# Two float32 additions of a recurrent graph layer moved from VectorE to TensorE, in a kernel whose instruction order is planned by searched leads

## The chip, the cores and the metric

The kernel runs on one core of a Trainium2 chip. The core has a tensor engine (PE, which multiplies matrices into PSUM), a vector engine (DVE), a scalar engine (ACT), GpSimd (POOL), and a sync engine (SP), which here only issues DMAs. Each engine works through its own queue in order; they wait for one another by semaphores. The metric is the device time of one execution in microseconds, lower is better. A profile of one execution gives the start and the duration of the instructions, the waits, and the clock that was granted to PE.

## The reference

Sixteen graphs of 1024 nodes with 64 features go through four layers, each of the form `x = x + layer(relu(layernorm(x)))`:

```python
# layer 0: two dense layers, a product with adj, and a recurrent (GRU) cell
msg = relu(adj @ m)
r, z = sigmoid(i_r + h_r), sigmoid(i_z + h_z)
n = tanh(i_n + r * h_n)
x = x + (1 - z) * n + z * h
# layer 1: normalized adjacency (adj + I), a dense layer, relu
# layer 2: each node's neighbours are thinned out by rank, and per feature a weighted sum
#          of three quantiles over the neighbours left is taken; then two dense layers
# layer 3: (adj + I) @ h, divided by the row sums
```

Layer 2 is the costly one: per node and feature the values of its neighbours have to be gathered and sorted. The change is in the last line of layer 0. With `h` the normalized input, the kernel computes it as `X + (n + z * (h - n))`.

## The kernel before

One graph is held as 8 tiles of 128 nodes. Python generators, one per stage and graph, issue the instructions. The stages are: `fetch` and `load` (read the adjacency, transpose it on PE, copy it to SBUF on ACT, write the transpose `adjT` to DRAM, take its signs), `code`, `rank`, `cut`, `list` (find degrees, rank the nodes by degree, thin the neighbours out, and make lists of neighbour indices), `mid` (layer 0, function `dense0`), `next` (layer 1, `dense1`, which ends by writing the table `tab` of normalized features to DRAM), `gath` (POOL's indirect DMAs fetch the neighbours' rows from `tab`), `sort` (sorting networks of minima and maxima on DVE for the 128 nodes of highest degree), `smalls` and `sums` (the same in two groups for the other seven tiles), and `rear` (`dense23`: the rest of layer 2, and layer 3).

POOL's gathers carry three names. The 26 `gh` gathers of a graph fetch the heavy nodes' neighbours into four buffers that come free only when PE has transposed them (`bank<-ident,gh`). The 49 `s` gathers (and 2 `px`) fill the light groups. The 8 `zz` gathers of the rear fetch a graph's aggregate `agg` back in node order; they stand in POOL's queue among the `s` gathers of the next graph, and wait until that graph's sorted sums are written. The `gh` gathers need the list `idxH` (a CAST on DVE) and the table `tab`.

The order of all this is written out by a planner, class `Order`. It keeps a clock per engine, a cost per instruction, and for each waiting stage the time at which its next step could start; the stage with the earliest start goes next. To that start a *lead* is added, in microseconds, from the table `LEAD`: per kind of stage five numbers for the engines V, A, T, P, S, one per graph index, and some for the first and the last graphs. The leads decide which stage's instructions come first in an engine's queue, and they come from a search. Since every queue is in order, an instruction that waits holds up all that stands behind it on its engine.

PSUM is handed out as four banks of 128x512 (`bank()`) and two double ones. A stage takes a bank, fills it from PE, and closes it when it is evicted.

All engine instructions are recorded through one helper, so the profile gives them all line 465; they are told apart by the names of their tiles: `hm` is `h` of layer 0, `nn` is `n`, `rz` holds `r` and `z`, `X` is the running `x` of the graph. The change is at the end of `dense0`. Around it:

```python
            yield "A", nn
            A.activation(nn, nn, AF.Tanh)
            yield "V", nn

            V.tensor_sub(h, h, nn)
            V.tensor_mul(h, h, rz[:, :, H : 2 * H])
            V.tensor_add(h, h, nn)
            V.tensor_add(X, X, h)
```

The first reader of the new `X` is `layernorm_relu` in `dense1`, which begins with a sum over the features on DVE (`ln_sn<-X`).

Of the kernel before, what the change touches and what calls it, by code (L numbers as in the profile page):

```python
# [156 lines left out]
def in_two_buffers(lens, kept, moves, first=None):  # L157
# [62 lines left out]


LEAD = {
    "rear": ((-0.25, -0.25, 0.25, -11, -65.5), -0, (0, -0, -0, -0), (-0.75, -6.5)),
    "gath": ((-11, 0, 0, -4.5, 0.25), -0, (-1.5, -0, 0, 0), (0, -0.25)),
    "sums": ((0, 0, 4, 21.75, -163.5), 0, (-0.75, 0, -0.75, 0), (0, 21.25)),
    "next": ((0, 0, 0, 14, 1.25), -0, (-0.5, 0, -0, 0), (0, 0)),
    "mid": ((0, -0, 0, 1, 4), 0, (-1, 0, -0, 0), (-0, 0)),
    "code": ((-192, -107.5, -0.25, 10, 0), 0, (5, 0, 1, -2), (3, 0)),
    "rank": ((0, 0, -121.5, 9.5, 7.75), 0, (-3.25, 0, 0, -0), (0, 0)),
    "cut": ((0, -1.25, -95.25, 0, -83.75), 0, (0, 0, 0, 0), (0, -0)),  # L230
    "list": ((-0, -3.5, -1, -10, -33.5), 0, (1, 0, -0, 0), (0, 0)),
    "fetch": ((-68.25, -2.25, -21.25, -29.5, -149.75), 0, (-10.5, -31.25, 0, -1.75), (2, 16)),
    "load": ((-49.75, 0, -163, -2.75, 1.25), 0, (-7.75, -0.5, 0, 0), (1, 1)),
    "sort": ((0, -79.5, -0.5, 21.25, -30.5), -0, (0, 0, 0, 0), (0.25, -0.75)),
    "smalls": ((0, 12.25, 7.5, 1.25, 1.5), 0, (0, 0, 0, 0), (-1.75, 1)),
    "flag": ((4, -17, -4.25, -1.75, -4.5), 0.1, (0, 8.5, 0, -8), (0, 0.75)),
    "keep": ((23, -0.75, 32.5, 4.25, -26), -1.55, (-9.75, -22.25, 7.25, 3.5), (15, 3.75)),
    "stream0": ((6, 0, 0, 2.5, -14.75), -0.15, (-9.25, 16.75, 0, 7.5), (-2.25, 2)),
    "stream1": ((8.75, -6, 11.25, 13.25, -2), 0.1, (3.5, 2.25, 0.75, -13.75), (-4.5, -5.75)),
    "stream3": ((-2.75, -4.75, -23, 1.75, -52.5), 1.5, (0.5, 0.5, 0, -6.25), (-27, -8.5)),  # L240
}


# [227 lines left out]
def kernel(  # L471
# [38 lines left out]
    ident = const.tile([P, P], F32, name="ident")  # L510
# [88 lines left out]
    def lists_for_all():  # L599
        order = Order(B)  # L600
        V, A, T = Engine(nc.vector, "V", order), Engine(nc.scalar, "A", order), Engine(nc.tensor, "T", order)
        G_, S_ = Engine(nc.gpsimd, "P", order), Engine(nc.sync, "S", order)

        def pool(name, bufs, **kw):
            return Pool(main.enter_context(tc.tile_pool(name=name, bufs=bufs, **kw)), order, bufs)
# [3 lines left out]
        ps1 = pool("ps1", 4, space=bass.MemoryType.PSUM)  # L609
        ps2 = pool("ps2", 2, space=bass.MemoryType.PSUM)  # L610

        def bank(dtype=F32):
            return ps1.take([P, 512 * 4 // mybir.dt.size(dtype)], dtype, "bank")
# [54 lines left out]
        for k in range(8):  # L668
            v = NBITS * 2.0**k
# [675 lines left out]
        def layernorm_relu(X, h=None, who="m", times=None):  # L1345

            yield "V", X
            s = wp.tile([P, NT], F32, name="ln_s" + who, bufs=2)
            V.reduce_sum(s, X, AX.X)
            yield "A", s  # L1350
            v = wp.tile([P, NT], F32, name="ln_v" + who, bufs=2)
            if h is None:
                h = wp.tile([P, NT, H], F32, name="h" + who, tag="h2r" if who == "r" else None, bufs=1)
            for t in range(NT):
                A.activation(h[:, t, :], X[:, t, :], AF.Square, bias=s[:, t : t + 1], scale=-float(H), accum_out=v[:, t : t + 1])
            A.activation(v, v, AF.Sqrt, bias=eps, scale=1.0 / H**3)
            yield "V", v
            V.reciprocal(v, v)
            if times is not None:
                V.tensor_mul(v, v, times)  # L1360
            V.scalar_tensor_tensor(s, s, -1.0 / H, v, ALU.mult, ALU.mult)
            yield "A", s, v
            for t in range(NT):
                A.activation(h[:, t, :], X[:, t, :], AF.Relu, bias=s[:, t : t + 1], scale=v[:, t : t + 1])
            return h
# [15 lines left out]
        def both(name, tag):  # L1381
            return wp.tile([P, N // 2], F32, name=name, tag=tag)

        def beside(on):
            T.beside = bool(on)

        def transposed(h, dst):
            yield "T", h
            pt = yield from bank()
            for t in range(4):  # L1390
                T.transpose(pt[:, t * P : (t + 1) * P], pair(h, t), ident)
            yield "A", pt
            for i in range(2):
                A.copy(dst[:, i * 512 : (i + 1) * 512], pt[i * H : (i + 1) * H, :])
            ps1.close(pt)
# [61 lines left out]
        def evicted(pm, dst, func=AF.Copy, bias=0.0):  # L1457
            yield "A", pm
            A.activation(dst, pm, func, bias=bias)
            ps1.close(pm)  # L1460
# [7 lines left out]
        def dense0(b, S):  # L1468
            S["X"] = X = wp.tile([P, NT, H], F32, name="X", bufs=2)
            S_.dma_start(X, x[b].rearrange("(t p) h -> p t h", p=P))  # L1470

            h = yield from layernorm_relu(X)
            cat = wp.tile([P, N], F32, name="cat")
            yield from transposed(h, cat[0:H, :])
            yield "T", cat
            m1T = both("m1T", "big")
            pm = yield from bank()
            for i in range(2):
                beside(i)
                T.matmul(  # L1480
                    pm[i * H : (i + 1) * H, :], w1, cat[0:H, i * 512 : (i + 1) * 512], start=True, stop=True
                )
            beside(0)
            yield from evicted(pm, m1T, AF.Relu, b1d)
            yield "T", m1T
            yield after(f"load{b}")
            p2 = yield from bank()
            T.matmul(p2, *bias(0), start=True, stop=False)
            ams = streamed(b, 0)
            for t in range(4):  # L1490
                T.matmul(
                    p2[:, t * P : (t + 1) * P], m1T[:, t * P : (t + 1) * P], w2d, start=False, stop=t == 3
                )
            yield "A", p2
            A.activation(m2x, p2.rearrange("p (t h) -> p t h", h=H), AF.Relu)
            ps1.close(p2)
            ps = yield from bank()
            pm = yield from propagated(b, m2x, 0, ams, sums=ps)

            yield "A", ps  # L1500
            m1T = wp.tile([P, 256], F32, name="sT", tag="big")
            A.copy(m1T, ps[:, 0:256])
            ps1.close(ps)
            yield "A", pm
            for i in range(2):
                A.activation(cat[H:P, i * 512 : (i + 1) * 512], pm[i * H : (i + 1) * H, :], AF.Relu)
            ps1.close(pm)
            yield "T", m1T
            pr = yield from bank()
            for c in range(2):  # L1510
                T.matmul(pr[:, c:NT:2], m1T[:, c * P : (c + 1) * P], pick, start=True, stop=True)
            yield "V", pr
            S["rs"] = rs = st.tile([P, NT], F32, name="rs")
            V.tensor_scalar(rs, pr[:, 0:NT], 1.0, None, ALU.add)
            ps1.close(pr)
            rz = wp.tile([P, NT, 2 * H], F32, name="rz", tag="big")
            nn = t2("nn")
            for g in range(2):
                yield "T", cat
                pg = yield from bank2()  # L1520
                for i in range(4):
                    t = 4 * g + i
                    o = pg[:, i * 4 * H : (i + 1) * 4 * H]
                    if i % 2 == 0:
                        T.matmul(pg[:, i * 4 * H : (i + 2) * 4 * H], *bias(2), start=True, stop=False)
                    c = (t % 2 * 4 + t // 2) * P
                    T.matmul(o, cat[:, c : c + P], wg, start=False, stop=i % 2 == 1)
                pgv = pg.rearrange("p (i c) -> p i c", c=4 * H)
                gs = slice(4 * g, 4 * g + 4)
                yield "A", pg  # L1530
                A.activation(rz[:, gs, :], pgv[:, :, 0 : 2 * H], AF.Sigmoid)
                yield "V", rz
                V.tensor_mul(nn[:, gs, :], pgv[:, :, 2 * H : G], rz[:, gs, 0:H])
                V.tensor_add(nn[:, gs, :], nn[:, gs, :], pgv[:, :, G : 4 * H])
                ps2.close(pg)
# [3 lines that stand above are left out]

            V.tensor_sub(h, h, nn)  # L1540
            V.tensor_mul(h, h, rz[:, :, H : 2 * H])
            V.tensor_add(h, h, nn)
            V.tensor_add(X, X, h)

        def dense1(b, S):
            X, rs = S["X"], S["rs"]
# [631 lines left out]
    ps1 = ctx.enter_context(tc.tile_pool(name="ps1", bufs=2, space=bass.MemoryType.PSUM))  # L2178
# [363 lines left out]
```

## Time and profile before

| | |
|---|---|
| median of 7 runs | 2278.94 us (2268.46 to 2289.73) |
| profiled execution | 2278.91 us, its span 2276.7 us |
| mean granted PE clock | 0.764 |
| DVE, ACT, POOL, PE busy | 84%, 68%, 67%, 67% of the span |
| first gather to last `s` gather | 155.1 to 2214.4 us from the span's start |

The span runs from the first to the last instruction of the profiled execution; the 2.2 us between it and that execution's time lie around it. An engine's busy share counts instructions that ran, not the time in which it issued a DMA or waited. In a line of a group the columns are: line, engine, operation, output and inputs with their shapes and the number of instructions, then busy time in all and mean nanoseconds of one, then the idle time just before them and what ended it. In a line of waits: who waited, for whom, microseconds in all, how often, and the longest. Numbers at the end of a tile's name are left out.

### The profile page before, as it was taken

Reading aid. Unit: us, or ns where it says so; the run is one execution under the profiler, and the core shown is the slowest. Engines: PE = TensorE matmul, PEld = TensorE weight load, DVE = VectorE, ACT = ScalarE, POOL = GpSimd, SP = SyncE. Lnnn points to the kernel's source line nnn. Section 1 sums busy time; section 2 is a strip of 40 time slices with the busy share of each in tenths; the row PEclk is TensorE's granted clock in tenths of the full one; section 3 lists DMA queues with packets and bytes.
Section 4 is the critical chain, followed back from the end, with each engine's and each line's share of the span. In section 5 each row is a group of like instructions: output and inputs, shape, how many; then the busy total and the mean of one; then the engine's idle time right before and its main releaser. Section 6 shows DMA issues by size and latency. Waiting matters only on the chain. (4 is left out here: it accounts for less than half of the span.)

```text
span 2276.7 us, 35564 instructions
## 1 busy us (share of the span) xinstructions
PE 1514.6 (67%) x9522; PEld 789.7 (35%) x9522; DVE 1907.2 (84%) x6317; ACT 1537.4 (68%) x5241; POOL 1519.0 (67%) x1428
## 2 busy tenths in 40 slices
PE   4876757676757677687876767766767685763324
PEld 3433334333333433333433433333333333331112
DVE  3547898898898988988997899888889899888982
ACT  5877776787777677787787668767866677554221
POOL 5017767567776776767676777677777677777771
PEclk9888778787678869797877787877777676775665
DMA  6767657677757667677767766766756565352341
GB/s 203 230 201 211 196 150 197 203 200 226 203 147 238 190 176 211 201 231 227 222 183 202 203 201 192 223 176 209 204 153 204 168 196 165 111 169 80 102 147 25
DMA packets 402724, 419.80 MB, mean 184 GB/s; under 512 B 176236, under 2 KB 313330, under 8 KB 402514
## 3 DMA queue, kind: packets, MB, share of 16 engines
q1 hardware_dynamic: 357426, 372.68, 53.1%
q0 software_dynamic: 45088, 44.75, 9.2%
q8 instruction: 78, 1.28, 0.2%
q14 instruction: 132, 1.08, 0.2%
HBM read 332.94 MB, written 84.34 MB: 183 GB/s over the span
## 5 line engine op out<-in xcount | busy, mean ns | idle before, releaser
L465 POOL DMA_INDIRECT s<-tab,idxL x784 | 863.8, 1102 | 239.0 <-issue 228.6
L465 POOL DMA_INDIRECT gh<-tab,idxH x416 | 445.0, 1070 | 343.9 <-DMA tab<-h 116.7
L465 DVE TENSOR_TENSOR hb<-hb 128x128 f32<-128x128 f32 (+10 forms) x1040 | 522.8, 538 | 16.3 <-ACT hb L465 11.7
L465 PE MATMUL bank<-ident,a 128*128 128x128 f32 x1024 | 196.5, 331 | 108.1 <-DMA a<-in_adj_dram 54.7
L465 POOL DMA_INDIRECT zz<-agg,posi x128 | 144.2, 1127 | 122.0 <-issue 47.2
L465 PE MATMUL bank<-am,tr 128*64 128x512 f32 x512 | 170.8, 780 | 74.0 <-ACT tr L465 37.1
L465 PE MATMUL bank<-am,hr 128*64 128x512 f32 x480 | 160.5, 777 | 74.5 <-ACT hr L465 41.7
L465 PE MATMUL bank<-am,m2x 128*64 128x512 f32 x512 | 165.5, 730 | 52.8 <-DMA am<-adjT 49.5
L465 PEld LDWEIGHTS bank<-ident,a 128*128 128x128 f32 x1024 | 143.2, 170 | 160.5 <-issue 46.6
L465 ACT COPY strip<-bank 128x512 f32<-128x512 f32 x256 | 146.6, 591 | 55.5 <-PE bank L465 43.5
L465 DVE TENSOR_TENSOR hb<-hb,hb 128x488 f32<-128x488 f32 (+7 forms) x368 | 173.4, 483 | 4.5
L465 ACT ACTIVATE s<-s,wl 128x64 f32<-128x64 f32 x624 | 166.5, 348 | 9.6 <-DVE s L465 9.6
L465 ACT ACTIVATE junk<-bank,nkey 128x1024 bf16<-128x1024 f32 x128 | 142.3, 1111 | 28.4 <-PE bank L465 26.2
L465 ACT ACTIVATE sgn<-strip,flat 128x1024 bf16<-128x1024 f32 x128 | 147.5, 1152 | 4.9 <-PE bank L465 1.8
L465 PE MATMUL bank<-cx,oh 128*128 128x133 f16 (+1 forms) x1280 | 143.2, 262 | 7.7 <-DVE oh L465 6.6
L465 PE MATMUL bank<-ident,gh 128*128 128x128 f32 x208 | 65.1, 340 | 120.0 <-DMA gh<-tab,idxH 103.7
L465 PEld LDWEIGHTS <-oh 128*128 128x128 f16 x1280 | 97.0, 109 | 47.0 <-issue 17.2
L465 DVE TENSOR_TENSOR o<-s 128x64 f32<-128x64 f32 (+6 forms) x208 | 95.1, 489 | 17.8 <-ACT s L465 10.4
L465 PE MATMUL bank<-wg,cat 128*128 128x256 f32 x256 | 94.2, 502 | 0.0
L465 DVE TENSOR_TENSOR s<-o 128x192 f32<-128x192 f32 (+5 forms) x224 | 94.0, 447 | 0.0
L465 PE MATMUL bank<-am,ones 128*32 128x256 f32 x1024 | 92.8, 438 | 0.0
L465 PEld LDWEIGHTS bank<-ident,gh 128*128 128x128 f32 x208 | 30.7, 158 | 175.8 <-issue 129.1
(443 smaller groups left out, 3742.9 us busy)
## 6 DMA issues: line engine op xcount, KB each, us to landing
am<-adjT SPq DMA_DIRECT2D x376, 512.0 KB
a<-in_adj_dram SPq DMA_DIRECT2D x128, 512.0 KB
adjT<-strip SPq DMA_DIRECT2D x128, 512.0 KB
s<-tab,idxL POOLq DMA_INDIRECT x784
gh<-tab,idxH POOLq DMA_INDIRECT x416
wb<-wd SPq DMA_DIRECT2D x32, 152.0 KB
X<-in_x_dram SPq DMA_DIRECT2D x16, 256.0 KB
x<-X SPq DMA_DIRECT2D x16, 256.0 KB
```

What stands on the lines that cost most here:

```text
L465: return f(*args, **kw)
```

## The change

The last two additions are no longer done on DVE. The stage waits until `X`, `nn` and `h` are ready for PE, takes a bank, and multiplies the identity with each of the three 128x512 tiles in turn, in float32, all three accumulated in that bank. ACT then copies the bank over `X`, and the bank is closed. The leads were searched anew, so the order of nearly everything else differs too: all 18 rows of `LEAD` have new numbers.

```diff
 LEAD = {
-    "rear": ((-0.25, -0.25, 0.25, -11, -65.5), -0, (0, -0, -0, -0), (-0.75, -6.5)),
-    "gath": ((-11, 0, 0, -4.5, 0.25), -0, (-1.5, -0, 0, 0), (0, -0.25)),
+    "rear": ((-0.25, -0.25, 0.25, -54, -111.25), 0, (0, -0, 0, 0), (-9, 1.5)),
+    "gath": ((-23, 0, 0, -8.5, 0), 0, (0, -1.5, 0, -0), (0.5, -1.25)),
...
-    "list": ((-0, -3.5, -1, -10, -33.5), 0, (1, 0, -0, 0), (0, 0)),
+    "list": ((0, -3.5, 0, -10.5, -95.75), 0, (0.75, 0, 0, -0), (0, 1.25)),
...
             V.tensor_sub(h, h, nn)
             V.tensor_mul(h, h, rz[:, :, H : 2 * H])
-            V.tensor_add(h, h, nn)
-            V.tensor_add(X, X, h)
+            yield "T", X, nn, h
+            px = yield from bank()
+            for i, v in enumerate((X, nn, h)):
+                T.matmul(px, ident, v.rearrange("p t h -> p (t h)"), start=i == 0, stop=i == 2)
+            yield "A", px
+            A.copy(X.rearrange("p t h -> p (t h)"), px)
+            ps1.close(px)
```

## The prediction

> **What bounds the kernel now.** I read the page first. No engine is full: DVE is busy for 84% of the span, the other three for about two thirds.
>
> ```profile
> span 2276.7 us, 35564 instructions
> PE 1514.6 (67%) x9522; PEld 789.7 (35%) x9522; DVE 1907.2 (84%) x6317; ACT 1537.4 (68%) x5241; POOL 1519.0 (67%) x1428
> ```
>
> POOL's share misleads, so the groups of instructions came next.
>
> ```profile
> L465 POOL DMA_INDIRECT s<-tab,idxL x784 | 863.8, 1102 | 239.0 <-issue 228.6
> L465 POOL DMA_INDIRECT gh<-tab,idxH x416 | 445.0, 1070 | 343.9 <-DMA tab<-h 116.7
> ...
> L465 POOL DMA_INDIRECT zz<-agg,posi x128 | 144.2, 1127 | 122.0 <-issue 47.2
> ```
>
> A gather takes 1.10 us and 0.30 us of issue follows it (228.6 over 750): 1.40 us each. In the timeline of POOL the first gather starts at 155.1 and the last `s` gather ends at 2214.4. Between them are 1352 gathers (416 gh, 784 s, 32 px, 120 zz), 1352 x 1.40 = 1895 us. The other 164 us are waits, and POOL's waits name them:
>
> ```profile
> POOL gh L465 <- PE bank L465: 100.9, 49, 11.7
> POOL zz L465 <- DMA agg<-s: 28.2, 3, 18.1
> POOL zz L465 <- DVE hb L465: 18.6, 4, 7.2
> POOL gh L465 <- DVE idxH L465: 12.1, 1, 12.1
> POOL zz L465 <- DVE ln_sn L465: 10.8, 1, 10.8
> ```
>
> By graph, from the gaps in POOL's timeline: gh waits 100.4 us, of which 3.9 in graph 0, 12.3 in graph 1, 12.1 where graph 2 waits for its list, 72.1 in the rest. The zz waits ahead of 2214.4 are 63.7 us (graphs 2 to 14). So span = 155.1 + 1895 + 164 + a tail of 62.3.
>
> Who paces the waits? I set the end of a graph's last `s` gather beside DVE's first min/max of its second light sort. For graphs 3 to 13 DVE comes 21 to 52 us late; for 14 and 15 only 3 and 2. It catches up once nothing is left to load, and then it waits for the gathers:
>
> ```profile
> 2215.92 1.76 DVE L465 TENSOR_TENSOR o<-s 128x768 f32<-128x768 f32 x3 [6.88 <-DMA s<-tab,idxL]
> ```
>
> The reader is to see three stretches: an opening up to the first gather of graph 2 (406.6), a middle up to graph 14 (1974.7) where POOL is ahead of DVE and waits for DVE and PE, and an end with only 3.5 us of POOL waits ahead of the tail, where gathers alone count.
>
> **The change part by part.** The profiled execution took 2278.91 us (span 2276.7 and 2.2 around it), 0.03 under the median of the seven runs. The sum is made against it.
>
> ```profile
> L465 DVE TENSOR_TENSOR hm<-hm,nn 128x512 f32<-128x512 f32 x32 | 22.0, 689 | 3.0 <-ACT nn L465 2.4
> L465 DVE TENSOR_TENSOR X<-X,hm 128x512 f32<-128x512 f32 x16 | 11.1, 692 | 0.5
> L465 PE MATMUL bank<-g,wkd 128*128 128x512 f32 x32 | 23.7, 831 | 8.0 <-ACT g L465 6.0 <-ACT u L465 1.7 <-ACT codes L465 0.2
> L465 ACT COPY strip<-bank 128x512 f32<-128x512 f32 x256 | 146.6, 591 | 55.5 <-PE bank L465 43.5 <-DMA adjT<-strip 11.2
> ```
>
> *Removed.* Two additions per graph, 0.69 + 0.69 = 1.38 us; 16 x 1.38 = 22.1 us of DVE. The twelve graphs of the middle hold 16.6 of it. The opening (DVE busy for 69.0 of its first 155 us) and the end give nothing.
>
> *Added on PE.* 48 products of 128x512 in float32 with a full array. The nearest row is `g,wkd`: two records per product, 23.7 / 16 = 1.48 us each. 48 x 1.48 = 71 us, 4.4 per graph; PE goes to about 1586 us, 70%.
> The Trainium skill (FP8 and Floating Point Precision, TensorE Precision Notes) counts four passes for a true float32 product; with the gap of N/2.4 + 2.5 ns at the full and N/1.2 at the half clock (TensorE: Matmul & The Clock Gate) I estimate 0.86 or 1.71 us, 41 or 82 us in all. The row lies between, at a mean granted clock of 0.764, and decides.
>
> *Added on ACT.* 16 evictions of 128x512, 0.59 us each: 9.5 us on an engine with 739 us idle. Taken as hidden; if ACT covers none of the middle's twelve, 7 us.
>
> *New waits.* The last product waits for DVE's multiplication; behind it on PE stand mostly the next transposes of `a`, and ACT's `strip` copies wait for those. The X copy waits for PE, and DVE's reduction `ln_sn<-X` for the copy: 1.48 + 0.59 us and hand-overs, some 2.6 us, or 5.5 if PE comes late to all three. Summing rows in issue order, the changed kernel has 2.5, 5.1 and 10.6 us of other DVE work in that place for graphs 0 to 2, and 7.9 to 65 after. So I cost it at nothing from graph 2 on; without that cover it is 12 x 5.5 = 66 us at most. The nearest PE wait for a DVE product, `bank <- DVE oc` (14.9 us in 7), prices PE's stalls at 0 to 2.1 us, 0 to 25 in the middle.
>
> *The order.* The leads move everything; I compared the issue orders.
> Opening: the CAST to idxH of graph 0, which the first gather needs, ran at 146.98. Now it stands behind graph 1's masking (`keys<-keys,own`). That took 33.6 us before, from the first `oh` (148.3) to `keys<-E,keys` (181.9). `oh` no longer stands behind that CAST and can start when ACT's last `junk` of graph 1 ends, 143.0 or some 6 us sooner as ACT's order moves it ahead of the LayerNorm squares. So idxH comes at about 171 and the first gather at 172: +17 (0 to +27). But graph 2 waited for its list until 406.6, and that list now stands behind 256 us of DVE work, not 269: about 392. POOL, 17 us late, ends graph 1 at 411 less what remains of 12.3 us of waits, 399 to 411. Graph 2 starts at its old time, -7 to +5; I take 0.
> Middle: a graph's light sums end 8 to 33 us of DVE work sooner (mean 17 for graphs 2 to 14) and its zz gathers stand 3.2 us of gathers later. Against each graph's zz wait that removes some 24 of the 63.7 us (0 to 63.7).
> PE: no new product falls between a graph's heavy transposes, but other PE work is bunched there. Beyond the 2.8 us of one column of gathers it grows from 103 to 152 us in graphs 2 to 15, beyond 5.6 us from 29 to 54. The 72 us of gh waits grow by 0 to 34 (x1.48) or to 62 (x1.86). I take 20.
> These two are no pace of their own: a gh wait gives DVE time, and a zz wait shrinks by it. What both must add up to is DVE's pace, so for the middle I take DVE's 16.6 us.
>
> Sum: 2278.9 + 0 (opening) - 16.6 (middle) + 0 (end) = 2262. It has a floor: DVE's `X<-X,u` of graph 15 stands behind 1748 us of DVE work (1747 before), and its table was sent 30 us before graph 15's first gather. Beyond 30 us, 2249, that gather waits.
>
> **The rivals.**
> *The late start stays (tie).* If graph 2 starts as late as graph 0, 2262 + 17 = 2279. For it: waits cannot shrink below what PE sets. Against: the 12.1 us for idxH, which need not come back.
> *PE paces the gathers (slower).* Place: gh, whose four buffers come free by transposes in PE's in-order queue. Price: +34 to +62, less at most 24 at zz: 2289 to 2317, about 2300. For it: 100.9 us of gh waits on PE, and 71 us more PE work. Against: in the order no product lies in those phases. It decides once gh waits of graphs 2 to 15 pass 72 + 16.6 + 11 = 100 us.
> *zz waits vanish too (faster).* 2278.9 - 63.7 would be 2215; the floor makes it 2249.
>
> The Trainium skill's own overview (Trainium Kernel Development and Optimization, Best Practices) warns that PSUM evacuation is not sped up by TensorE. It speaks against a detour through PSUM; if ACT bound, the evictions would replace 22.1 us by 9.5 and the gain would be 12.6, 2266. ACT's 68% does not bear that out.
>
> **How the numbers follow.** Forecast 0.46 (2252 to 2273; 0.38 of it under 2267.5), zz waits gone 0.08, late start 0.16, PE 0.30. About 0.5%, 11 us, is what a measurement can tell: faster 0.38 + 0.08 = 0.46, same 0.08 + 0.13 + 0.03 = 0.24, slower 0.03 + 0.27 = 0.30. The range reaches from the floor to PE's 2300: 2247 to 2300.
>
> **What would show it.** Right: DVE near 1885 us; PE near 1586; first gather near 172, graph 2's first near 407; zz waits near 40; gh waits (graphs 2 to 15) under 100; `ln_sn<-X` hardly waiting for ACT's X copy; graph 14 starting some 16 us sooner. Wrong: a product far from 1.48 us, a first gather later than 182, or a new long wait for a table or list.

## The result, and the profile after

The changed kernel takes 2284.59 us (median of 29 runs, 2273.99 to 2292.32); the kernel before took 2275.21 (71 runs, 2255.21 to 2297.54). The ratio is 1.0039, with a 95% interval of 1.0026 to 1.0052: slower by 9 us, where 2262 had been forecast. That is still inside the 0.5% that the prediction called "same", but on the wrong side, and the interval leaves no doubt of the sign. Here and below, ratios and their intervals compare fast runs alone and are not the quotients of the medians beside them.

The profiled execution of the changed kernel took 2271.17 us, less than any of its 29 timed runs, and that of the kernel before 2278.91. So the two profiles show how the work moved, but not the 9 us, and the experiments below are needed for the sum. The page of the changed kernel, its span and engines:

```profile
span 2269.1 us, 35709 instructions
...
PE 1534.3 (68%) x9618; PEld 783.2 (35%) x9618; DVE 1889.4 (83%) x6285; ACT 1544.0 (68%) x5257; POOL 1517.8 (67%) x1428
```

DVE lost 17.8 us of the 22.1 forecast. PE gained 19.7 and not 71, but its granted clock differs, 0.789 against 0.764. The groups of the changed kernel, by form, show the change itself:

```profile
L465 PE MATMUL bank<-X,ident 128*128 128x512 f32 x32 | 24.1, 846 | 1.2 <-ACT y L465 1.2
...
L465 PE MATMUL bank<-nn,ident 128*128 128x512 f32 x32 | 22.5, 795 | 1.0 <-ACT nn L465 1.0
...
L465 PE MATMUL bank<-hm,ident 128*128 128x512 f32 x32 | 17.1, 615 | 1.0 <-DVE hm L465 1.0
...
L465 ACT COPY X<-bank 128x512 f32<-128x512 f32 x16 | 9.3, 583 | 10.5 <-PE bank L465 10.5
```

There are two records per product, so 63.7 us in 48 products: 1.33 us each. The products themselves hardly wait, and `ln_sn` never waits for the copy: no line of DVE's waits names it. PE does, though, for the bank that the copy has to empty first (PE's waits, changed kernel):

```profile
PE bank L465 <- ACT X L465: 9.0, 2, 8.7
```

The long one is in graph 8: its products end at 1044.8, ACT copies their bank at 1054.7, behind other work, and PE's next product (`cmask,onesh`, whose inputs are constants) waits from 1046.6 to 1055.3.

POOL's waits, changed kernel:

```profile
POOL gh L465 <- DVE nz L465: 136.4, 2, 135.5
POOL gh L465 <- PE bank L465: 136.1, 59, 20.5
...
POOL zz L465 <- DMA agg<-s: 19.9, 2, 18.7
...
POOL zz L465 <- DVE oh L465: 8.0, 4, 4.7
```

The first line is nearly all the opening, up to the first gather; of the zz waits on `agg`, 18.4 us lie in the tail. By graph, from the gaps in POOL's timeline, the zz waits of graphs 2 to 14 fell from 63.7 to 13.4 us and the gh waits of graphs 2 to 15 rose from 84.2 (the 72.1 of the prediction and the 12.1 for `idxH`) to 112.4. The new order trades one wait for the other. The first gather starts at 174.1 (155.1 before), graph 2's at 403.5 (406.6), graph 14's at 1963.5 (1974.7), and the last `s` gather ends at 2198.5 (2214.4). Up to here the profiled execution is 16 us ahead. From there to the end it takes 70.6 us instead of 62.3.

That tail is new. `u` is the last tile that DVE computes for the output. In the timeline of the changed kernel the last `u` is followed by the sums of the flags, a small stage (`marked`) that counts how many graphs need a repair path; none does here:

```profile
2254.08 0.20 PE L465 MATMUL bank<-flags,ones_col 128*1 128x16 f32 x2
2254.36 0.35 DVE L465 SCALAR_TENSOR_TENSOR u<-bank,rd,Xr 128x64 f32<-128x64 f32 x2
2254.63 0.15 DVE L465 CAST flag_i<-bank 1x16 int32<-1x16 f32 x1
2254.71 0.15 DVE L465 TENSOR_REDUCE tot<-bank 1x1 f32<-1x16 f32 x1
...
2254.89 0.14 DVE L465 CAST flag_i<-tot 1x1 int32<-1x1 f32 x1
```

In the timeline of the kernel before the same instructions stood ahead of the last zz gathers, under 45 us of other work:

```profile
2225.12 0.21 PE L465 MATMUL bank<-flags,ones_col 128*1 128x16 f32 x2 [33.56 <-DVE flags L465]
2225.37 0.16 DVE L465 CAST flag_i<-bank 1x16 int32<-1x16 f32 x1 [0.40 <-PE bank L465]
...
2225.65 0.14 DVE L465 CAST flag_i<-tot 1x1 int32<-1x1 f32 x1
```

Every engine reads the count before it ends. The view of that source line has, for POOL, in the kernel before:

```profile
L2486 POOLq TENSOR_LOAD <-flag_i x1: 507/507/507, 2235.4 to 2235.4; - x1
```

and in the changed kernel:

```profile
L2491 POOLq TENSOR_LOAD <-flag_i x1: 510/510/510, 2255.1 to 2255.1; - x1
```

POOL's next long record, from the trace's list of all records (start and duration in us), is a closing DRAIN:

```
kernel before    last u ends 2271.2   POOL DRAIN 2238.89 12.41   end 2276.7
changed kernel   last u ends 2254.7   POOL DRAIN 2259.16  9.14   end 2269.1
```

Before, the drain had ended 20 us ahead of the end of the last `u`. In the changed kernel it starts 4.5 us after it, and the program ends 14.4 us after the last `u`, not 5.5. That is 8.9 us, the size of the whole loss. Whether it is the loss, the first experiment asks.

### The profile page after: what moved, and what is told of

Same layout as the page of the kernel before. It is cut to its first block, busy times and chain, and to the rows that moved or that the text cites. A ratio compares the mean times of both kernels' runs of the same rounds, so it can differ in the third digit from the quotient of the medians.

```text
span 2269.1 us, 35709 instructions
## 1 busy us (share of the span) xinstructions
PE 1534.3 (68%) x9618; PEld 783.2 (35%) x9618; DVE 1889.4 (83%) x6285; ACT 1544.0 (68%) x5257; POOL 1517.8 (67%) x1428
## 4 chain that ended last, share of the span: by engine, by line
DVE 15%; PE 13%; DMA 11%; ACT 7%; POOL 6%; issue 4%; SPq 3%; DVEq 0%; POOLq 0%; ACTq 0%
PE bank L465 13%; DVE hb L465 6%; DMA am<-adjT 4%; DMA gh<-tab,idxH 4%; POOL gh L465 3%; SPq L465 3%; POOL s L465 2%; DVE o L465 2%; DVE s L465 2%; POOL zz L465 1%; ACT hr L465 1%; DMA s<-tab,idxL 1%; ACT s L465 1%; ACT u L465 1%; DMA X<-in_x_dram 1%
## 5 line engine op out<-in xcount | busy, mean ns | idle before, releaser
L465 POOL DMA_INDIRECT gh<-tab,idxH x416 | 451.9, 1086 | 380.9 <-DVE nz L465 136.4
L465 PE MATMUL bank<-am,tr 128*64 128x512 f32 x512 | 175.8, 802 | 61.7 <-ACT tr L465 32.8
L465 PE MATMUL bank<-am,hr 128*64 128x512 f32 x480 | 169.2, 817 | 69.9 <-DMA am<-adjT 37.5
L465 PE MATMUL bank<-am,m2x 128*64 128x512 f32 x512 | 156.4, 692 | 56.4 <-DMA am<-adjT 46.4
L465 PEld LDWEIGHTS bank<-ident,a 128*128 128x128 f32 x1024 | 137.4, 166 | 164.2 <-ACT strip L465 55.9
L465 PE MATMUL bank<-ident,gh 128*128 128x128 f32 x208 | 64.5, 351 | 123.6 <-DMA gh<-tab,idxH 118.9
L465 PE MATMUL bank<-cx,oh 128*128 128x133 f16 (+1 forms) x1280 | 129.6, 248 | 2.1 <-DVE oh L465 1.2
L465 PEld LDWEIGHTS <-oh 128*128 128x128 f16 x1280 | 89.7, 104 | 36.5 <-issue 15.6
L465 ACT ACTIVATE cx<-bank 128x128 f16<-128x128 f32 (+1 forms) x192 | 51.9, 313 | 73.0 <-PE bank L465 65.7
L465 ACT COPY hb<-bank 128x128 f32<-128x128 f32 (+13 forms) x240 | 43.9, 282 | 72.3 <-PE bank L465 72.1
```

The lines of the kernel that those rows point to most:

```text
L465: return f(*args, **kw)
```

## The experiments

Each kernel below keeps the order of the kernel that it is made from, instruction for instruction on every queue, apart from the edit. Where work is left out, the planner was still charged for it (`planned` in the diffs does only that), so that nothing else moves. The first four kernels ran in one set, 12 times each against 35 runs of the kernel before, which took 2278 us there, its usual time. In the five later sets the kernel before itself took 3066 to 3140 us (on three other chips, and in the last set on the very chip that had run it in 2278), so ratios of those sets hold for that condition alone.

**The flags, both ways round.** One row of the leads is exchanged:

```diff
-    "flag": ((13.5, 1.75, -4.5, 4.75, -21.25), 0.15, (29, 16.5, 0, 10), (-10.5, 13)),
+    "flag": ((4, -17, -4.25, -1.75, -4.5), 0.1, (0, 8.5, 0, -8), (0, 0.75)),
```

> The changed kernel with the old numbers in one row of the leads, that of the stage which sums the flags; the whole order stays but for this stage, whose product, three DVE instructions and DMA go back ahead of the last graph's zz transposes. In the changed kernel's trace the four engines read the flag count at 2255.07, and POOL's closing DRAIN then takes 9.14 us (2259.16 to 2268.30), so the last `u` at 2254.7 is followed by 14.4 us; before it was 5.5 us. Theory (the moved flags are what made the kernel slower): 2284.6 - 8.9 = about 2276, level with the 2275.2 of before. Rival (the loss is made in the middle, by the gh waits on PE, which grew from 72 to 112 us in graphs 2 to 15): 2283 to 2285, no change against the changed kernel.

Measured: 2279.03 us, ratio to the kernel before 0.9996 (0.9970 to 1.0021): the theory's tie, and the interval excludes the rival.

> The kernel before with the new numbers in the row of the flags alone: the stage that sums the flags now stands last, behind the last `u`; nothing else moves. Theory (flags): 2275.2 + 8.9 = about 2284, a ratio of 1.004. Rival (the loss is made in the middle): 2275, ratio 1.000.

Measured: 2286.95 us against 2277.97, ratio 1.0040 (1.0015 to 1.0065). The same three records as above:

```
before, flags late     last u ends 2265.0   POOL DRAIN 2270.68  9.14   end 2280.6
changed, flags early   last u ends 2275.4   POOL DRAIN 2243.69 12.51   end 2281.5
```

From the last `s` gather to the end the four profiles have 62.3 us (before), 70.6 (changed), 62.2 (changed, flags early) and 71.5 (before, flags late). So one stage of a handful of instructions, put last, costs 0.4% in either kernel. Within these intervals it is the whole loss, and with the flags back the change is a tie.

**The additions taken away.** Is the gain of the middle there to be had?

```diff
-            V.tensor_add(h, h, nn)
-            V.tensor_add(X, X, h)
+            planned(V, "tensor_add", [h], [h, nn])
+            planned(V, "tensor_add", [X], [X, h])
```

> The kernel before, its order kept instruction for instruction, without the 32 additions: the last two additions of the recurrent layer are left out, X stays as it was. DVE loses 22.1 us, 16.6 of it in graphs 2 to 13. Theory of the prediction (DVE paces the middle): 2275.2 - 16.6 = about 2259. Rival (the gathers, PE or others pace the middle as well, so DVE's time is not passed on): 2270 to 2275.

Measured: 2277.11 us against 2277.97, ratio 0.9986 (0.9959 to 1.0014). That is 3 us, and at most 9 by the interval; 16.6 is outside it, and the time lies near the rival's. The stretch that the prediction called the middle, from graph 2's first gather to graph 14's, as windows (length, busy time of PE, PEld, DVE, ACT and POOL with instruction counts, granted clock, DMA share, GB/s). The kernel before:

```profile
406.60:1974.70 1568.10, 1113.19 (x6989) 574.09 (x6988) 1397.77 (x4552) 1130.66 (x3886) 1124.22 (x1021) 0.78 0.67 197
```

The kernel before without the additions:

```profile
410.40:1975.50 1565.10, 1115.27 (x6993) 575.19 (x6992) 1382.53 (x4528) 1130.46 (x3886) 1126.73 (x1020) 0.78 0.69 197
```

DVE works 15 us less and the stretch is 3 us shorter, no more than the same order with late flags has by chance (1564.3). In DVE's waits over these windows, summed by engine, 144.1 us became 156.9: waits on PE 18.1 to 28.5, waits on ACT 118.6 to 119.8. The largest one on ACT, and the one on PE that grew most, before:

```profile
DVE u L465 <- ACT u L465: 36.0, 11, 7.9
...
DVE idxH L465 <- PE bank L465: 3.9, 3, 1.6
```

and without the additions:

```profile
DVE u L465 <- ACT u L465: 33.3, 12, 7.2
DVE idxH L465 <- PE bank L465: 15.5, 5, 3.7
```

Most of what DVE no longer computes, it waits.

**The products taken away.** The changed kernel with the flags early, without the products; ACT copies `hm` over `X`, so PE no longer waits for that copy to empty a bank either:

```diff
-                T.matmul(px, ident, v.rearrange("p t h -> p (t h)"), start=i == 0, stop=i == 2)
+                planned(T, "matmul", [px], [ident, v.rearrange("p t h -> p (t h)")])
...
-            A.copy(X.rearrange("p t h -> p (t h)"), px)
+            planned(A, "copy", [X.rearrange("p t h -> p (t h)")], [px])
+            A.engine.copy(X.rearrange("p t h -> p (t h)"), h.rearrange("p t h -> p (t h)"))
```

> The changed kernel with the flags early, its order kept instruction for instruction, without the 48 products: ACT copies `hm` over `X` where it copied the bank, so X and n are left out of the sum. PE loses 63.7 us. Theory (the products take the gain of the middle through PE, by the gh waits): some 10 to 17 us faster than the same kernel with its products, 2259 to 2266, and gh waits of graphs 2 to 15 back near 72 us. Rival (the products lie beside other work): within 4 us of it, about 2276.

Measured: 2272.49 us, ratio 0.9985 (0.9964 to 1.0007); 6.5 us under the same order with its products by the medians, 2.5 by the two ratios, whose intervals overlap. The theory's 10 to 17 us did not come. PE has 57 us less (1488.5 against 1545.5). POOL's wait on PE with the products (changed kernel, flags early):

```profile
POOL gh L465 <- PE bank L465: 141.4, 59, 21.1
```

and without them:

```profile
POOL gh L465 <- PE bank L465: 139.7, 68, 21.1
```

The gh waits stay (122.6 and 118.9 us in graphs 2 to 15). They were expected back near 72 if the products made them. They come with the new order; products and bank together cost the end some 3 to 7 us, if anything.

**New order, additions on DVE.** The new leads without the change of engines (flags early; two additions on DVE behind the multiplication, no products, no copy).

```diff
             V.tensor_mul(h, h, rz[:, :, H : 2 * H])
+            V.engine.tensor_add(h, h, nn)
+            V.engine.tensor_add(X, X, h)
...
-                T.matmul(px, ident, v.rearrange("p t h -> p (t h)"), start=i == 0, stop=i == 2)
+                planned(T, "matmul", [px], [ident, v.rearrange("p t h -> p (t h)")])
...
-            A.copy(X.rearrange("p t h -> p (t h)"), px)
+            planned(A, "copy", [X.rearrange("p t h -> p (t h)")], [px])
```

> The order of the changed kernel with the flags early, instruction for instruction, but the two additions done by DVE as before, behind the multiplication, and neither products nor bank nor ACT copy: the new leads without the change of engines. The same order with the products took 2279.0, without products and additions 2272.5. Theory of the prediction (DVE paces the middle): 2272.5 + 16.6 = about 2289, so the move to TensorE is worth some 10 us in its own order. Theory after the last runs (taking 22 us from DVE gave nothing before, so DVE does not pace): 2272 to 2276, and the move itself costs 3 to 7 us.

> The new order with the additions on DVE once more, on a chip that runs the kernel before in its usual time, if this is one: on the last chip it took 3077 us, with PE idle for 325 us at issue, and the ratios there say little of the usual chip. Theory of the prediction (DVE paces the middle): b1 was 2272.5 without additions, so about 2289, ratio 1.005. Theory since the first runs (DVE's 22 us are not passed on): 2272 to 2276, ratio 0.997 to 0.999, as 0.999 on the slow chip.

> New order, flags early, additions on DVE, on a usual chip. Theory of the prediction (DVE paces the middle): 2272.5 + 16.6 = about 2289, so that the move is worth 10 us in its own order. Theory since (DVE's 22 us are not passed on): 2270 to 2277, the move itself worth nothing or less.

> New order, flags early, additions on DVE. On a usual chip: 2289, ratio 1.005, if DVE paced the middle; 2270 to 2277, ratio 0.997 to 0.999, if DVE's time is not passed on. The three sets on slow chips gave 0.999, 1.008 and 1.001.

Measured, in this order: 3072.94 us against 3077.10, ratio 0.9992 (0.9954 to 1.0031); 3081.23 against 3066.19, 1.0081 (1.0041 to 1.0121); 3072.67 against 3081.69, 1.0009 (0.9954 to 1.0064); 3154.24 against 3138.78, 1.0020 (0.9974 to 1.0066). None is at the usual time, so what the move is worth in its own order stays open. They only say that in that condition the new order is no better than the old one when both do the additions on DVE.

**Products twice.** Each product issued a second time into the same bank, 48 more (flags early).

```diff
+            for i, v in enumerate((X, nn, h)):
+                T.engine.matmul(px, ident, v.rearrange("p t h -> p (t h)"), start=i == 0, stop=i == 2)
```

> The changed kernel with the flags early and every one of the three products issued twice into the same bank, the second set in place of the first: 48 products more on PE, 64 us, nothing else moved. If PE's time is passed on in part, as the 6.5 us between the runs with and without products say: +6 to +10, about 2286 to 2289. Rival (each stall of PE is passed on whole, through the four gh buffers): +30 or more, 2310. Rival (products lie beside other work, the 6.5 us were scatter): within 3 us of 2279.

> The products issued twice, 64 us more of PE, on a usual chip. If PE's time is passed on in part, as the 6.5 us between the runs with and without products say: +6 to +10 against 2279, ratio 1.003 to 1.005. If each stall is passed on whole: +30 or more, ratio 1.013. If products lie beside other work: ratio 1.000. On the slow chip it was 1.0085.

> Products issued twice, 64 us more of PE. On a usual chip: ratio 1.003 to 1.005 if PE's time is passed on in part, as with and without products (6.5 us for 64); 1.013 or more if every stall is passed on; 1.000 if products lie beside other work. The two sets on slow chips gave 1.009 and 1.012.

Measured: 3102.09 us against 3077.10, ratio 1.0085 (1.0047 to 1.0124); 3093.71 against 3066.19, 1.0116 (1.0063 to 1.0169); 3160.77 against 3138.78, 1.0086 (1.0054 to 1.0118). So it is 0.9 to 1.2% above the kernel before. The kernel that this one is made from did not run in these sets; against the new order with the additions on DVE, in the same three sets, it is 0.9, 0.4 and 0.7% by the ratios. PE's time seems to reach the end there, but how much of that is the second set of products is not shown, and no run at the usual time shows it.

**Seven gh buffers.** POOL may run 3 columns (of two gathers each) further ahead of PE's transposes; the planner still counts four buffers. For room, two constants of the repair path are made there instead of at the start.

```diff
-                    ghs[c] = qp.tile([P, 2, H], F32, name="gh", bufs=GH)
+                    ghs[c] = qp.tile([P, 2, H], F32, name="gh", bufs=GH, real=7)
...
```

> The changed kernel with the flags early, its order kept, and seven buffers for the gh gathers instead of four (room from two constants of the repair path, which are made there now). POOL may run 3 columns of gathers, 8.4 us, further ahead of PE's transposes. Theory (gh waits on PE are what replaced DVE's gain, POOL paces): most of the 120 us of gh waits in graphs 2 to 15 go, at least half of it, and the time falls by 20 to 60 us, to 2220 to 2260. Rival (the waits only move: what stands behind, the sorts on DVE and the zz gathers, is no sooner): gh waits fall, zz and other waits grow by as much, 2270 to 2279.

> Seven gh buffers in the changed kernel with the flags early, on a usual chip. Theory (gh waits on PE replaced DVE's gain, POOL paces): 20 to 60 us faster than 2279. Rival (the waits only move to the zz gathers and the sorts): 2270 to 2279. Second rival, from the slow chip, where it was 3.5% slower: gathers that run further ahead take DMA time from the loads of adjT, and the time rises, 2290 or more.

> Seven gh buffers, changed kernel with the flags early, for a chip on which the kernel before takes its usual 2275 us. Theory (gathers pace, held up by the gh buffers): 20 to 60 us faster than 2279. Rival (no engine paces alone; the sorts and zz gathers behind come no sooner): 2270 to 2285 while the gh waits on PE fall. Second rival, as on the two slow chips: 2 to 4% slower, by waits of the zz gathers that grow more than the gh waits fall.

> Seven gh buffers, changed kernel with the flags early. On a usual chip: 20 to 60 us under 2279 if gathers pace; 2270 to 2285 if no engine paces alone; 2 to 4% slower if what the slow chips showed (zz waits grow more than gh waits fall) holds there too.

Measured, changed kernel: 3182.76 us, ratio 1.0353 (1.0319 to 1.0387); 3183.00, 1.0399 (1.0353 to 1.0446); 3168.52, 1.0361 (1.0284 to 1.0437); 3249.93 against 3140.24, 1.0413 (1.0330 to 1.0496).

> The same seven gh buffers in the kernel before, its order kept. gh waits of graphs 2 to 15 were 72 us on PE. Theory (POOL paces): 15 to 40 us faster, 2235 to 2260. Rival (the waits move to zz and to DVE): 2268 to 2278.

> Seven gh buffers in the kernel before, on a usual chip. Theory (POOL paces): 15 to 40 us faster, 2235 to 2260. Rival (the waits move): 2268 to 2278. Second rival (the gathers ahead cost the loads their time, 2.6% slower on the slow chip): 2290 or more.

> Seven gh buffers in the kernel before, on a usual chip. Theory (gathers pace): 15 to 40 us faster. Rival (no engine paces alone): 2268 to 2282. Second rival, as on the slow chips: some 2% slower.

Measured, kernel before: 3154.88 us, ratio 1.0258 (1.0214 to 1.0301); 3147.72, 1.0217 (1.0139 to 1.0295); 3154.31, 1.0328 (1.0249 to 1.0407). The waits moved as the rivals had it: in the changed kernel's first run POOL's gh waits on PE are 208.6 us and its zz waits (without issue) 572.7. The two runs of the same set that have the new order and four buffers show 368.9 and 360.6 (additions on DVE), 387.5 and 362.6 (products twice). The last section has what this condition does to a kernel whose gathers stream. No run shows whether the buffers would help at the usual time.

## Why the prediction was wrong

*The end, costed at "0 (end)": wrong, and it decides the sign.* The sum kept the tail of 62.3 us as it was. It followed the leads of the opening and the middle, but not the row of the flags, although that row changed too and its three DVE instructions stand behind the last `u` in the issue order. The trace before held a hint of the price: a drain of 12.4 us, which ended 20 us ahead of the last `u` and so cost nothing. Once its start stands behind the last `u`, 8.9 us of it show. None of the rivals named it, and none of the signs that were to show the prediction wrong was one for the end. That 2284.6 lies inside the range of 2247 to 2300 is luck: the upper end stood for PE pacing the gathers, which is not what made the kernel slower.

*The middle, "for the middle I take DVE's 16.6 us": wrong.* 0.14% (3 us, at most 9) came of it when the additions were simply left out. The step that failed is the one before: that DVE paces because its second light sort starts 21 to 52 us after the gathers that feed it. Late against the gathers is not the same as working without a break. In those 1568 us DVE itself waited 144, 118.6 of them for ACT, and that was in the trace before. In such waits a saving can be lost, and here it was: 15 us less work, 13 us more waiting. Over the two orders the middle took 1568.1 and 1564.3 us (before, and with late flags) and 1560.0 and 1575.7 (changed, and with early flags): the same mean within 2 us; without the additions it took 1565.1, without the products 1554.9. So the sign "graph 14 starting some 16 us sooner" told nothing: it came 11 us sooner in the changed kernel's profile and 7 us later with early flags. Which resource does pace the middle is not settled; neither taking DVE's 22 us away nor taking the products' 64 away shortened the run by a like amount.

*PE.* A product was taken at 1.48 us and measured 1.33; 63.7 us in all instead of 71. The row `g,wkd` that it was taken from, the same work in both kernels, went from 23.7 to 18.5 us itself, with mean granted clocks of 0.764 and 0.789, so a single row carries an error of this size. The Trainium skill's passes (FP8 and Floating Point Precision, TensorE Precision Notes) with its gap between matmuls (TensorE: Matmul & The Clock Gate, Back-to-back issue gap) had given an estimate of 0.86 or 1.71 us; the measured value lies between these, at a mean granted clock of 0.789. "gh waits under 100" failed with 112, and by the text that was the point from which the rival "PE paces the gathers" decides. But its mechanism did not hold: without any product the gh waits stay at 118.9, and with early flags the kernel is level at 2279, not at 2289 to 2317. The warning on PSUM that the prediction quotes is about tiling on TensorE, while the products here use the whole array (128*128), and ACT was not bound: its 16 copies took 9.3 us.

*zz waits.* Forecast to fall by 24 to about 40, they fell to 13. The sum of gh waits (graphs 2 to 15) and zz waits (2 to 14) is 147.9 before, 125.8 in the changed kernel and 135.1 with early flags; 134.0 in the kernel before with late flags. The text had said that the two are no pace of their own and that a gain in one is taken by the other. That was right in the main: zz waits fell by 50, gh waits rose by 28, and the better reading would have been to take nothing for either. (1352 x 1.40 is 1893, not 1895; nothing in the forecast hangs on it.)

*Opening and new waits: right but for one wait.* First gather at 174.1 (forecast 172), graph 2's at 403.5 (forecast 407, less 7 to plus 5): the late start is absorbed. No reader waits for the X copy, and ACT grew by 7 us. PE's stalls were priced by products that wait for DVE, "0 to 25 in the middle", and those came to nothing (1.0 us on `hm`); the stall that did come, 9.0 us for the bank until it is copied, was not thought of. No run takes it away alone, so what it costs is not shown.

## What to carry to other kernels

When a whole table of priorities is exchanged, follow every row to its place in the issue order, the small stages at the end of the program first: a handful of instructions whose result every engine must read before it ends cost nothing under other work here and 0.4% behind it. Before a saving on a busy engine is counted, sum that engine's own waits in the same stretch, or leave the work out in an otherwise unchanged order; here one run showed that these additions were worth some 3 us and not 16.6. And two profiles of one order (but for the flags) differed by 16 us over the middle, so a difference of 8 us between two kernels' profiles, which here even had the wrong sign, is no result.

## What the runs showed of the hardware

POOL's closing DRAIN took 9.14 us when it began 32 us after the last gather had ended (changed kernel) and 34 us after it (before with late flags). In the kernel before it began 3.3 us ahead of that end, at 2238.89 against 2242.16, and took 12.41: it was over 9.14 us after the gather ended. With early flags it is the same sum, 2247.06 + 9.14 = 2256.20. Without products (2228.11, over at 2237.26) and without additions (2239.22, 2248.36) it comes to 9.14 or 9.15 again. So in these six traces it costs 9.14 us after whichever is later, the last gather or the engine's arrival at its end, even where the last gather had ended 32 us before.

In the sets at 3066 to 3250 us the work of DVE and ACT took hardly longer (new order with additions on DVE: DVE 1912.4 us, ACT 1540.9), but in stretches where POOL streamed `s` gathers without a pause they nearly stood still. One such stretch, as a window, in the new order with additions on DVE at 3072.94 us:

```profile
215.50:281.10 65.60, 15.40 (x66) 6.27 (x62) 5.17 (x7) 11.62 (x36) 50.06 (x52) 0.58 0.33 87
```

and in the changed kernel with early flags at 2279.03 us the stretch that begins with the same gathers and holds nine more:

```profile
209.20:294.10 84.90, 64.96 (x386) 29.65 (x383) 67.80 (x205) 62.45 (x179) 66.61 (x61) 0.83 0.80 233
```

DVE is busy for 8% of the first and 80% of the second. Summed over all `s` gathers between 200 us and graph 15's first gather, DVE was busy for 38% of their time in the one and 88% in the other; over the gh gathers, which pause at their buffers, for 87% and 88%. That would fit that both kernels with seven buffers, which pause less, were 2 to 4% slower there than the kernel before, but it is not shown to be the cause, and what holds the other engines back was not found: the profile names no releaser for much of that idle time (325.1 us of PE's waits, against 0.3).
